# Expert results sent to two rows of each token as slots end, combined by whole-block loads

## The chip, the cores and the metric

The kernel runs on one core of a Trainium2 chip. The metric is device time in microseconds, the median of several executions. One execution was also profiled; its trace gives every instruction's start, length and wait. PE is the matrix engine (PEld its weight loads), DVE the vector engine, ACT the scalar engine, POOL GpSimd and SP the engine that here only issues DMAs.

## The reference, cut to what matters

`x` is 2 x 4096 tokens of 256 floats. An attention-like layer (projections, a decaying running sum, a gate) is added to `x` and normalised; then each token goes through two of eight experts:

```python
x = _layernorm(x + _L0_attn_ref(x, ...))
# _L0_ffn_ref, on the flattened tokens:
logits = x_flat @ gate_W                       # 8 experts
gates = jax.nn.softmax(logits, axis=-1)
tk_g, tk_i = jax.lax.top_k(gates, TOP_K)       # the two best
tk_g = tk_g / (jnp.sum(tk_g, axis=-1, keepdims=True) + 1e-08)
cw = jnp.sum(jax.nn.one_hot(tk_i, E, dtype=x.dtype) * tk_g[..., None], axis=1)
out = x_flat
for e in range(E):
    h = jax.nn.relu(x_flat @ W1[e] + b1[e])    # 256 -> 512
    out = out + cw[:, e:e + 1] * (h @ W2[e] + b2[e])
x = _layernorm(x + out)                        # out begins with x_flat: x counts twice
```

## The kernel before, in words

Tokens are worked in 16 blocks of 512 (`NB`; a block is 4 parts of 128 tokens, `NT`). `attention(i)` (L291) is a generator that does one block in steps; the main loop at the end of the program interleaves the steps of three neighbouring blocks and puts expert work between them (`fill`). PE, DVE, ACT and SP run exactly in the order in which the Python program emits (`IN_ORDER`); POOL's order is made by the scheduler, but each POOL instruction, too, waits for those ahead of it.

A block's first layer ends in `rr` (L358 to L378): attention output plus input, normalised to `x1`, which ACT's queue also stores in HBM as `x1_dram[i]` (L377). A normalisation takes its power -0.5 on POOL (`rstd_of`, L233 to L239, the power is L238): DVE prepares the variance (L237), POOL raises it, DVE and ACT go on. There are 32 such powers in the attention part (`rstd_y`, `rstd_a`) and 16 at the end (`rstd_f`).

The routing part finds each token's two experts (`largest`, L411), counts tokens by expert (L451), and computes for each token and choice a row number in `xs`, a buffer in HBM where each expert has a region of its own. Eight indirect DMAs on POOL (L470) send the block's x1 rows there, one per part and choice, 128 rows of 1 KB each.

The blocks form two groups, 13 and 3 (`GROUPS`). As soon as regions fill, `plan_slots` (L496) plans "slots": 256 consecutive rows of one expert, and once a group is complete, 21 "rest" slots of 128 rows, some of them padding. Group 0 has 45 full slots and 21 rest slots, group 1 has 5 and 21. A slot goes through:

- `load_slot` (L559 on): SP loads the rows (`xg`, L571) and the expert's first weights (`w`, 512 KB, L578), up to three slots ahead;
- `slot_columns`: PE transposes the rows (L590), DVE copies them (`xgT`, L591), ACT copies the expert's second weights from the resident `kept` (L596);
- `slot_first` (L608, ReLU on ACT at L615) and `slot_second` (L629, bias added by DVE at L633 into `ysl`, two buffers);
- `store_slot` (L638): SP stores `ysl` into `ys`, at the same rows as in `xs`.

`half()` does half of this for one slot; `store_slot` comes one half after the slot's result.

When all slots of a group have been stored, its blocks are combined. `gather` (L644 on) loads a part's two expert rows per token by two indirect DMAs on POOL (L654) with the row numbers kept from the routing, and, at a block's first part, SP loads x1 (`sum`, L650). `AHEAD = 3` parts are gathered before one is weighed. `weigh` (DVE) adds both rows times their weights (L669, two instructions) and takes statistics (L675, L676). Then `scale_of` (power on POOL) and `end`: DVE `less` (L687), four ACT instructions (L689), and a store of the block (L693). `some_combining(n)` does n such steps; `half()` sets n in proportion to what is left, so that group 0's combination is spread over group 1's slots. After the last slot only combination is left.

At the start POOL zero-fills padding areas: 14 DMAs of 128 rows (L205) and, when a group is complete, 8 more each after the regions' ends. `lam_sb` holds the decay spread over 512 columns for the running sum (L302), made by two copies (L761).

Of the kernel before, what the change touches and what calls it, by code (L numbers as in the profile page):

```python
# [15 lines left out]
P = 128  # L16
# [4 lines left out]
AHEAD = 3  # L21
# [10 lines left out]
def kernel(  # L32
# [22 lines left out]

    nc = tc.nc
# [18 lines left out]
    KEPT = NF * D + D + NF  # L75
# [5 lines left out]
    lam_sb = const.tile([P, NC, TB], FP, tag="lam", name="lam_sb")  # L81
# [43 lines left out]
    kept = const.tile([P, E, KEPT], FP, tag="kept", name="kept")  # L125

# [29 lines left out]
    m_rows = const.tile([1, MAXS, E], FP, tag="m_rows", name="m_rows")  # L156
    nc.vector.tensor_scalar_mul(m_rows, m_tab, float(SL))

    zeros = const.tile([P, D], FP, tag="zeros", name="zeros")
    nc.gpsimd.memset(zeros, 0.0)  # L160

    class Group:


        def __init__(self, k, n_blocks):
# [7 lines left out]
            self.xs = dram.tile([rows, D], FP, tag=f"xs_{k}", name=f"xs_{k}")  # L173
            self.ys = dram.tile([rows, D], FP, tag=f"ys_{k}", name=f"ys_{k}")
# [10 lines left out]
            self.dumps = const.tile([1, MAXS, E], FP, tag=f"dumps_{k}", name=f"dumps_{k}")  # L185
            nc.vector.tensor_scalar(
                self.dumps, m_tab, float(E - 1 - self.rest), 0.0, ALU.add, ALU.max
# [6 lines left out]
                self.off, m_tab, float(P), self.dumps, ALU.mult, ALU.subtract  # L194
# [9 lines left out]
        def put_zeros(self, row):  # L204
            self.put(nc.gpsimd.dma_start(  # L205
                out=self.xs[ds(row, P), :], in_=zeros
            ))
# [7 lines left out]
        def store(self, dma):  # L215
            key = f"ys_{self.k}"

            tc.declare_no_dep(
                dma.ins, group=key, keep=self.stored[-1:], reason="rows of their own"
            )  # L220
            tc.add_to_no_dep_group(key, dma.ins)
            self.stored.append(dma.ins)

    groups = [Group(k, n) for k, n in enumerate(GROUPS)]
    for m in range(E - 1):
        for gr in groups:
            gr.put_zeros(gr.dump + m * P)
# [45 lines left out]
    def project(w, xT, o, name):  # L273
# [13 lines left out]
        dram.tile([P, NT, D], FP, tag=f"x1_{i}", name=f"x1d_{i}") for i in range(NB)  # L287
# [3 lines left out]
    def attention(i):  # L291
# [7 lines left out]
        for o in range(NC):  # L299
# [4 lines left out]
                lam_sb[:, o, :],  # L304
# [53 lines left out]
        rr = work.tile([P, NT, D], FP, tag="x1", name=f"x1_{i}", bufs=3)  # L358
        for t2 in range(NT // 2):
            o_ps = ps_a.tile([P, 2, D], FP, tag="pa", name=f"ao_{i}_{t2}")  # L360
            for u in range(2):
# [6 lines left out]
                rr[:, 2 * t2 : 2 * t2 + 2, :], o_ps, x_t[:, 2 * t2 : 2 * t2 + 2, :], ALU.add  # L368
# [3 lines left out]
        mv = row_stats(lambda t: rr[:, t, :], f"a{i}")  # L372
        r = rstd_of(mv[:, :, 1:2], f"a{i}")
        yield
        normalise(x1, lambda t: rr[:, t, :], mv, r, f"a{i}")
# [35 lines left out]
        def largest(src, name, hot):  # L411
# [9 lines left out]
            return top  # L421

        hot = small.tile([P, 2, NT, E], FP, tag="hot", name=f"hot_{i}")
        top1 = largest(g, "1", hot[:, 0])
# [3 lines left out]
        top2 = largest(rest, "2", hot[:, 1])  # L428
# [50 lines left out]
    def schedule(gr, j):  # L479
# [3 lines left out]
        if j == gr.n_blocks - 1:  # L483

            ends = small.tile([1, E], I32, tag="s_ends", name=f"ends_{gr.k}")
            nc.vector.tensor_copy(ends, gr.base[:1, :])
            for e in range(E):
                gr.put_zeros(
                    nc.values_load(
                        ends[:, e : e + 1], engines=[ENG.Pool],  # L490
                        min_val=e * gr.cap, max_val=(e + 1) * gr.cap - P,
                    )
                )
            plan_slots(gr, f"{gr.k}_rest", gr.rest, True)

    def plan_slots(gr, name, n, rest):  # L496
# [52 lines left out]
        if rest:  # L549
            nc.vector.tensor_tensor(plan[:, 0, :n, :], at, gr.dumps[:, :n, 0:1], ALU.add)  # L550
        else:
            nc.vector.tensor_copy(plan[:, 0, :n, :], at)
# [7 lines left out]
    def load_slot(s):  # L560
# [8 lines left out]
        xg = slot.tile([P, SL // P, D], FP, tag="xg", name=f"xg_{name}", bufs=3)  # L569
# [13 lines left out]
    def slot_columns(s):  # L583
# [7 lines left out]
        nc.vector.tensor_copy(xgT, pt)  # L591
        e = nc.values_load(
# [4 lines left out]
        return gr, name, size, row, xgT, w1_t, wb[:, 0, :]  # L597

    def slot_first(s):
        gr, name, size, row, xgT, w1_t, wb = s  # L600
        b1_t = wb[:, NF * D + D :]
# [16 lines left out]
        return gr, name, size, row, hT, wb  # L618

    def slot_second(s):  # L620
        gr, name, size, row, hT, wb = s
# [12 lines left out]
        return gr, size, row, y  # L634

    def store_slot(s):
        gr, size, row, y = s
        gr.store(nc.sync.dma_start(  # L638
            out=gr.ys[ds(row, size), :].rearrange("(p t) d -> p t d", p=P), in_=y
        ))  # L640
        left[gr.k] -= size // P
        if left[gr.k] == 0:
            to_gather.extend((i, t) for i in place if place[i][0] is gr for t in range(NT))

    def gather(i, t):

        gr, _ = place[i]
        if t == 0:
            sums[i] = work.tile([P, NT, D], FP, tag="sum", name=f"sum_{i}", bufs=3)
            nc.sync.dma_start(out=sums[i], in_=x1_dram[i])  # L650
        both = []
        for k in range(2):
            yk = work.tile([P, D], FP, tag=f"y{k}", name=f"y{k}_{i}_{t}", bufs=AHEAD + 2)
            dma = nc.gpsimd.indirect_dma_start(  # L654
                out=yk.bitcast(I32),
                out_offset=None,
                in_=gr.ys.bitcast(I32),
                in_offset=bass.IndirectOffsetOnAxis(ap=poss[i][:, k, t, :], axis=0),
            )
            for ins in gr.stored:  # L660
                tc.add_manual_dep(dma.ins, ins.name, SYNC, reason="rows stored before")
            both.append(yk)
        return i, t, both

    def weigh(i, t, both):
# [183 lines left out]
```

## Time and profile before

| what | value |
|---|---|
| median of 3 executions | 1097.53 us (1095.64 to 1101.23) |
| the profiled execution's own time | 1091.48 us |
| its span, first to last instruction | 1089.5 us |
| PE busy | 899.7 us, 83% |
| DVE busy | 548.4 us, 50% |
| ACT busy | 386.1 us, 35% |
| POOL busy | 318.5 us, 29% |
| moved by DMA | 163.79 MB, 150 GB/s over the span |
| L470, indirect DMA out of x1 | 128 times, 972 ns each on POOL |
| L654, indirect DMA into y | 128 times, 981 ns each on POOL |
| L669, weighing, DVE | 128 times, 481 ns each |
| L238, power, POOL | about 1.0 us each |
| L633, `ysl`, DVE | 686 ns for a full slot |

"Busy" is the time in which the engine worked; for POOL's indirect DMAs it is the time to issue them, not that of the transfer. A row of the groups by line gives line, engine, operation, output and inputs, count, then busy time and mean duration, then the engine's idle time before and what ended it. In the timeline a line gives start, length, engine, line, operation and, in brackets, idle time before it and what ended that.

### The profile page before, as it was taken

The page shows a single profiled execution, that of the slowest core. Times are in us where ns is not written, and L with a number is a line of the kernel's source. Part 1 is how long each engine was busy: PE and PEld are TensorE (multiplying, and loading weights), DVE is VectorE, ACT ScalarE, POOL GpSimd, SP SyncE. Part 2 cuts the span into 40 slices and gives each one's busy share as a digit, 9 for nine tenths or more (in the row PEclk, how much of TensorE's full clock was granted, in tenths as well). Part 3 has the DMA queues.
Part 4 walks back from the last instruction along what each step waited for, and adds up shares of the span by engine and source line. Part 5 has one row for each costly group of instructions (what it writes and reads, how often), then busy time and mean ns, then how long its engine had stood idle before and what let it go on. Part 6 is the DMA issues. An engine that isn't in the chain of part 4 may idle for free. (4 is left out here: it accounts for less than half of the span.)

```text
span 1089.5 us, 14838 instructions
## 1 busy us (share of the span) xinstructions
PE 899.7 (83%) x4366; PEld 713.7 (66%) x4366; DVE 548.4 (50%) x1841; ACT 386.1 (35%) x733; POOL 318.5 (29%) x346
## 2 busy tenths in 40 slices
PE   4988586899899999999999999999898965776710
PEld 2555354778677777778786868688797854666610
DVE  2675544356455554555455455534334245665544
ACT  1221212323333334343333323334454423554412
POOL 3112321302030303030211203130304367676454
PEclk9998796999999999999999999999899988888965
DMA  5611214232333424242434342443647857988653
GB/s 192 205 54 44 88 60 143 99 124 88 133 119 126 151 101 161 94 151 88 146 102 131 112 131 97 164 155 128 193 155 226 269 182 246 281 296 267 229 175 110
DMA packets 95041, 163.79 MB, mean 150 GB/s; under 512 B 12081, under 2 KB 45361, under 8 KB 94961
## 3 DMA queue, kind: packets, MB, share of 16 engines
q1 hardware_dynamic: 68800, 107.52, 30.6%
q0 software_dynamic: 13728, 37.50, 10.4%
q10 hardware_dynamic: 12432, 17.84, 4.5%
q8 instruction: 34, 0.56, 0.2%
q14 instruction: 47, 0.38, 0.1%
HBM read 106.72 MB, written 56.10 MB: 149 GB/s over the span
## 5 line engine op out<-in xcount | busy, mean ns | idle before, releaser
L629 PE MATMUL po<-wb,hT 128*128 128x256 f32 x800 | 190.3, 393 | 8.1 <-issue 6.2
L608 PE MATMUL ph<-xgT,w 128*128 128x256 f32 x800 | 185.8, 386 | 10.4 <-DVE xgT L591 10.4
L608 PEld LDWEIGHTS ph<-xgT,w 128*128 128x128 f32 x800 | 154.1, 194 | 36.9 <-DVE xgT L591 11.2
L629 PEld LDWEIGHTS po<-wb,hT 128*128 128x128 f32 x800 | 153.6, 197 | 29.7 <-issue 7.1
L470 POOL DMA_INDIRECT xs<-x,pos x128 | 124.4, 972 | 142.8 <-DVE rows L512 102.1
L615 ACT ACTIVATE hT<-ph,wb 128x256 f32<-128x256 f32 x200 | 83.9, 471 | 211.3 <-PE ph L608 149.8
L654 POOL DMA_INDIRECT y<-ys,pos x128 | 125.5, 981 | 81.3 <-issue 29.9
L238 POOL TENSOR_TENSOR rstd_a<-rstd_a,half_neg 128x4 f32<-128x4 f32 x16 | 16.1, 1007 | 429.5 <-DVE rstd_a L237 429.5
L629 PE MATMUL po_rest<-wb_rest,hT_rest 128*128 128x256 f32 x336 | 89.6, 415 | 18.0 <-DVE rstd_f L237 12.8
L608 PE MATMUL ph_rest<-xgT_rest,w_rest 128*128 128x128 f32 x672 | 89.3, 290 | 18.2 <-DVE xgT_rest L591 12.4
L591 DVE COPY xgT<-xt 128x512 f32<-128x512 f32 x50 | 34.5, 691 | 137.1 <-PE xt L590 110.1
L608 PEld LDWEIGHTS ph_rest<-xgT_rest,w_rest 128*128 128x128 f32 x672 | 86.9, 204 | 24.1 <-DVE xgT_rest L591 14.2
L615 ACT ACTIVATE hT_rest<-ph_rest,wb_rest 128x128 f32<-128x128 f32 x168 | 48.1, 369 | 116.3 <-PE ph_rest L608 45.8
L629 PEld LDWEIGHTS po_rest<-wb_rest,hT_rest 128*128 128x128 f32 x336 | 67.0, 210 | 29.1 <-issue 16.3
L633 DVE TENSOR_TENSOR ysl<-po,wb 128x512 f32<-128x512 f32 x50 | 34.3, 686 | 85.9 <-PE po L629 33.5
L276 PE MATMUL g<-xT,wg_sb 128*128 128x512 f32 x128 | 61.4, 621 | 8.4 <-DVE state L302 5.0
L596 ACT COPY wb<-kept 128x1284 f32 x50 | 63.1, 1262 | 3.8 <-DVE ysl L633 0.9
L669 DVE SCALAR_TENSOR_TENSOR sum<-y,wt,sum 128x256 f32<-128x256 f32 x128 | 61.5, 481 | 5.5 <-DMA y<-ys,pos 3.3
L276 PE MATMUL q<-xT,wq_sb 128*128 128x512 f32 x128 | 59.7, 610 | 0.4 <-ACT yg L351 0.4
L276 PE MATMUL v<-xT,wv_sb 128*128 128x512 f32 x128 | 59.5, 609 | 0.3 <-issue 0.3
L363 PE MATMUL ao<-wo_sb,yg 128*128 128x256 f32 x256 | 58.2, 380 | 0.9 <-DVE y L326 0.9
L596 ACT COPY wb_rest<-kept 128x1284 f32 x42 | 53.5, 1275 | 5.0 <-DVE ysl_rest L633 3.6
(143 smaller groups left out, 1097.9 us busy)
## 6 DMA issues: line engine op xcount, KB each, us to landing
w<-in_w_dram SPq DMA_DIRECT2D x50, 512.0 KB
w_rest<-in_w_dram SPq DMA_DIRECT2D x42, 512.0 KB
xg<-xs SPq DMA_DIRECT2D x50, 256.0 KB
ys<-ysl SPq DMA_DIRECT2D x50, 256.0 KB
x<-in_x_dram SPq DMA_DIRECT2D x16, 512.0 KB
x1d<-x ACTq DMA_DIRECT2D x16, 512.0 KB
sum<-x1d SPq DMA_DIRECT2D x16, 512.0 KB
out_dram<-sum ACTq DMA_DIRECT2D x16, 512.0 KB
```

The source lines that it names most:

```text
L238: nc.gpsimd.tensor_tensor(r, r, half_neg[:, :n, :], ALU.pow)
L276: last = nc.tensor.matmul(ps, w[:, c, ts(o, P)], xT[:, c, :], start=(c == 0), stop=(c == NC - 1))
L363: nc.tensor.matmul(o_ps[:, u, :], yg[:, c, ts(2 * t2 + u, P)], wo_sb[:, c, :], start=(c == 0), stop=(c == NC - 1),)
L470: gr.put(nc.gpsimd.indirect_dma_start(out=gr.xs, out_offset=bass.IndirectOffsetOnAxis(ap=pos[:, k, t, :], axis=0), in_=x1s[i][:, t, :], in ...
L591: nc.vector.tensor_copy(xgT, pt)
L596: nc.scalar.copy(wb, kept[:, ds(e, 1), :])
L608: nc.tensor.matmul(ph[:, u, :], w1_t[:, c, ts(f0 + u, P)], xgT[:, c, :], start=(c == 0), stop=(c == NC - 1),)
L615: nc.scalar.activation(hT[:, f, :], ph[:, u, :], AF.Relu, bias=b1_t[:, f : f + 1])
L629: nc.tensor.matmul(po[:, t, :], hT[:, f, ts(t, P)], w2_t[:, f, :], start=(f == 0), stop=(f == NF - 1),)
L633: nc.vector.tensor_tensor(y, po, b2_t.broadcast_to([P, n_t, D]), ALU.add)
L654: dma = nc.gpsimd.indirect_dma_start(out=yk.bitcast(I32), out_offset=None, in_=gr.ys.bitcast(I32), in_offset=bass.IndirectOffsetOnAxis(ap= ...
L669: nc.vector.scalar_tensor_tensor(x1[:, t, :], yk, wt[:, k, t, :], x1[:, t, :], ALU.mult, ALU.add)
```

## The change

Each row in `xs` now carries eight more floats (`ROW = D + 8`, 1056 bytes). Float 0 of them is twice the token's number in its group, float 1 tells the token's first expert as `E - e`. The first is written by DVE for each block (from a table made once by POOL), the second is a copy in the routing part. `x1_dram` has the wide rows too. `xs`, its padding included, holds valid numbers everywhere: padding rows carry numbers of spare rows behind the tokens' own. The spare rows are made once in HBM (`no_rows`) and copied from there; filling at the start takes six larger POOL DMAs in place of 14.

`ys` has two rows for each token, first and second choice reversed (`1 - k` at weighing). A slot copies the two floats out of `xg` (`whose`, DVE), and after its result computes the target row (`to`, DVE): twice the token's number, plus one if the slot's expert is the token's first. `kept` has one more float per expert for that comparison. `store_slot` sends the result by indirect DMAs on POOL, one per 128 rows, and no longer through SP.

`gather` is gone. `load_sum` loads, for a whole block, x1 and both rows of each token by two plain DMAs on SP, the second of 1 MB after all stores of the group. It does so while at most one block is waiting to be weighed, with two buffers for the rows. The pace is computed with a load as one step.

`lam_sb` is gone; the running sum reads one column repeated. Tables of the planner are smaller.

```diff
+    ROW = D + 8
-    KEPT = NF * D + D + NF
+    KEPT = NF * D + D + NF + 1
...
+    for e in range(E):
+        nc.vector.memset(kept[:, e, KEPT - 1 :], float(E - e))
...
+    def put_none(rows, k, n):
+        rows = rows.rearrange("(n p) d -> p n d", p=P)
+        return (
+            nc.gpsimd.dma_start(out=rows[:, :, :D], in_=zeros.broadcast_to([P, n, D])),
+            nc.gpsimd.dma_start(out=rows[:, :, D:], in_=none[:, k : k + n, :]),
+        )
+    no_rows = dram.tile([E * P, ROW], FP, tag="no_rows", name="no_rows")
+    put_none(no_rows, 0, E)
...
-        def put_zeros(self, row):
-            self.put(nc.gpsimd.dma_start(
-                out=self.xs[ds(row, P), :], in_=zeros
-            ))
+        def put_none(self, row, e):
+            self.put(nc.gpsimd.dma_start(out=self.xs[ds(row, P), :], in_=no_rows[ts(e, P), :]))
...
-            tc.declare_no_dep(
-                dma.ins, group=key, keep=self.stored[-1:], reason="rows of their own"
-            )
+            tc.declare_no_dep(dma.ins, group=key, reason="rows of their own")
...
-                lam_sb[:, o, :],
+                lam_col[:, o : o + 1].broadcast_to([P, TB]),
...
+        rr = work.tile([P, NT, ROW], FP, tag="x1", name=f"x1_{i}", bufs=3)
+        nc.vector.tensor_scalar_add(rr[:, :, D:], number, float(2 * TB * place[i][1]))
...
+        top1, first = largest(g, "1", hot[:, 0])
+        nc.vector.tensor_copy(x1[:, :, D + 1 : D + 2], first)
...
         nc.vector.tensor_copy(xgT, pt)
+        whose = slot.tile([P, SL // P, 2], FP, tag="whose", name=f"whose_{name}", bufs=4)
+        whose = whose[:, : size // P, :]
+        nc.vector.tensor_copy(whose, xg[:, : size // P, D : D + 2])
...
         nc.vector.tensor_tensor(y, po, b2_t.broadcast_to([P, n_t, D]), ALU.add)
-        return gr, size, row, y
+        to = slot.tile([P, SL // P, 1], I32, tag="to", name=f"to_{name}")[:, :n_t, :]
+        nc.vector.scalar_tensor_tensor(
+            to, whose[:, :, 1:2], wb[:, KEPT - 1 :], whose[:, :, 0:1], ALU.is_equal, ALU.add
+        )
+        return gr, size, to, y
...
-        gr.store(nc.sync.dma_start(
-            out=gr.ys[ds(row, size), :].rearrange("(p t) d -> p t d", p=P), in_=y
-        ))
+        for t in range(size // P):
+            gr.store(nc.gpsimd.indirect_dma_start(
+                out=gr.ys,
+                out_offset=bass.IndirectOffsetOnAxis(ap=to[:, t, :], axis=0),
+                in_=y[:, t, :],
+                in_offset=None,
+            ))
...
-    def gather(i, t):
...
+    def load_sum(i):
+        gr, j = place[i]
+        x1 = work.tile([P, NT, ROW], FP, tag="sum", name=f"sum_{i}", bufs=3)
+        nc.sync.dma_start(out=x1, in_=x1_dram[i])
+        y2 = work.tile([P, NT, 2, D], FP, tag="y2", name=f"y2_{i}")
+        dma = nc.sync.dma_start(
+            out=y2,
+            in_=gr.ys[ts(j, 2 * TB), :].rearrange("(t p k) d -> p t k d", t=NT, p=P),
+        )
+        for name in gr.stored:
+            tc.add_manual_dep(dma.ins, name, SYNC, reason="rows stored before")
+        sums[i] = x1
+        to_weigh.extend((i, t, y2) for t in range(NT))
...
-            if to_gather:
-                gathered.append(gather(*to_gather.pop(0)))
-            if len(gathered) > AHEAD or (gathered and not to_gather):
-                weigh(*gathered.pop(0))
+            if to_load and len(to_weigh) <= NT:
+                load_sum(to_load.pop(0))
+            elif to_weigh:
+                weigh(*to_weigh.pop(0))
...
-        debt[0] += len(to_gather) * size / (P * max(1, 2 * sum(left.values()) - 8))
+        todo = 5 * len(to_load) + len(to_weigh)
+        debt[0] += todo * size / (P * max(1, 2 * sum(left.values()) - 8))
```

## The prediction, made before the changed kernel ran

> **What bounds the kernel now.** I read the stretches first, since the program has stages with different limits (columns: the stretch and its length, busy us and instruction count of PE, PE's weight loads, DVE, ACT and POOL, then granted clock, DMA share, GB/s).
>
> ```profile
> 300.00:600.00 300.00, 288.92 (x1386) 228.40 (x1385) 157.67 (x549) 108.02 (x193) 58.87 (x60) 1.00 0.37 124
> 600.00:830.00 230.00, 214.85 (x1167) 182.75 (x1166) 109.51 (x409) 92.70 (x180) 50.98 (x56) 0.97 0.44 145
> 860.00:890.00 30.00, 20.97 (x88) 17.52 (x87) 11.75 (x31) 7.15 (x14) 19.98 (x21) 0.83 0.64 212
> 920.00:950.00 30.00, 18.46 (x104) 15.68 (x102) 14.79 (x42) 13.21 (x28) 21.06 (x21) 0.86 0.87 283
> 950.00:980.00 30.00, 22.17 (x117) 19.25 (x118) 19.39 (x56) 17.48 (x37) 20.87 (x21) 0.80 0.86 281
> 1010.00:1040.00 30.00, 23.38 (x140) 20.46 (x138) 14.86 (x42) 13.78 (x30) 12.02 (x12) 0.94 0.57 189
> 1040.00:1089.50 49.50, 0.00 (x0) 0.00 (x0) 23.94 (x70) 10.37 (x20) 27.64 (x28) 0.54 0.48 151
> ```
>
> Three stages. Up to about 857 us ("front") PE is 93 to 96% busy and nothing near the change can give more than a few per cent. From 857 to 1040 ("window") group 0's blocks are combined beside group 1's slots: PE works only 126.6 of 180 us (the six 30-us stretches summed) and DMA is the fullest resource, 0.84 to 0.87 in the middle. From 1040 ("tail") PE has ended; 49.5 us go to group 1's combination.
>
> The groups by line, then the tail's timeline, tell what the tail waits for:
>
> ```profile
> L470 POOL DMA_INDIRECT xs<-x,pos x128 | 124.4, 972 | 142.8 <-DVE rows L512 102.1
> L654 POOL DMA_INDIRECT y<-ys,pos x128 | 125.5, 981 | 81.3 <-issue 29.9
> L669 DVE SCALAR_TENSOR_TENSOR sum<-y,wt,sum 128x256 f32<-128x256 f32 x128 | 61.5, 481 | 5.5 <-DMA y<-ys,pos 3.3
> ```
> ```profile
> 1042.79 1.01 POOL L654 DMA_INDIRECT y<-ys,pos  x1 [12.96 <-DMA ys<-ysl_rest]
> 1044.10 0.97 POOL L654 DMA_INDIRECT y<-ys,pos  x1 [0.30 <-issue]
> ...
> 1046.40 0.48 DVE L669 SCALAR_TENSOR_TENSOR sum<-y,wt,sum 128x256 f32<-128x256 f32 x1 [1.35 <-DMA y<-ys,pos]
> ...
> 1082.79 2.07 ACT L689 ACTIVATE sum<-sum,less,rstd_f 128x256 f32<-128x256 f32 x4 [4.23 <-DVE less L687]
> ```
>
> A gather occupies POOL 0.96 us and the next follows 0.30 us later, 1.26 us each. 24 of them are 30 us of the tail, and DVE follows at their pace. In the window 104 gathers are 131 us of POOL, while SP's own waits name the store:
>
> ```profile
> SPq L638 <- DVE ysl_rest L633: 14.3, 8, 2.8
> SPq L638 <- DMA ys<-ysl_rest: 7.8, 7, 2.3
> ```
>
> All waits of L638 there sum to 35.8 us (14.3, 7.8, 6.2, 3.0, 1.9, 1.7, 0.9), with later weight and row loads queued behind it on SP. The window also opens with a hole: PE's transpose at 879.62 waited 7.14 us for rows whose load SP issued at 857.81, while 14 gathers were issued.
>
> **What the Trainium skill says.** "DMA: Bandwidth & Descriptors", section "Issuing engines are not separate DMA queues": transfers of SP, ACT and POOL run on the same 16 engines and interleave. The trace agrees: in 860 to 1040 the three queues take 41.6, 25.1 and 9.1% of them, so a gather replaced by a plain load of the same bytes frees POOL, not DMA. Same page, "Anatomy of one DMA — SWDGE (gpsimd) path": a small DMA's time is mostly its receipt. Here a gather's rows are used 2.2 to 2.6 us after its issue ended (1045.07 to 1047.26 and 1043.80 to 1046.40). Same page, "Measured (HBM→SBUF, 128 partitions, SWDGE, issued from GpSimd)": 1 MB from HBM takes 6.15 us; no 1 MB load is in this trace, whose best short stretches move 340 to 350 GB/s. Same page, "How a descriptor splits into AXI transactions": an unaligned start costs extra beats, up to 7 on the 33 of a 1056-byte row; no such row is in the trace of before.
>
> **The change part by part.** Account: span 1089.5 us, execution 1091.5 us, 6 us under the median of 1097.5; I carry differences over to the median.
>
> *Tail, removed and added.* Removed are 24 gathers. Added: the last scatter and three block loads. The last slot's result is ready at 1040.0. The row number on DVE (like L687, 0.17 us), a scatter on POOL (0.96, the row of L470), landing 2.4 us (middle of the gathers'), SP's issue 0.4: the first block's rows start at 1044.0. Block load 6 us (the page's price; 4.5 to 8, from 350 GB/s plus landing, up to sharing with the x1 load): 1050.0. One part of a block on DVE takes 1.57 us in the tail (two of L669, statistics 0.43 and 0.18, gaps), a block 6.3: block 13 ends at 1056.3. Block 14 was loaded behind it: ends 1062.6. Block 15 reuses block 13's buffer (two are kept), so its load starts at 1056.4 and lands at 1062.7: ends 1069.0. Variance, power, `less` 1.5; then ACT and the last store as now (1082.79 to 1089.5, 6.7): 1077.2. Gain 12 us, 8 to 16 with the load's bounds.
>
> *Window.* Bytes stay: 104 gathers of 128 KB become 13 block loads of 1 MB; the stores become scatters of equal size; x1 and xs rows grow by 3%. One block's share is about 1.05 (y) + 0.54 (x1) + 0.52 (out) + 2.1 slots of 0.79 MB = 3.8 MB, at 283 GB/s 13.3 us; it now takes 180/13 = 13.8. DVE's part per block is 6.3 + 2.6 (slots) + waiting for the power; about 12 us, so DMA stays the bound. What can improve is filling: SP no longer waits in L638, its loads come earlier, and slot results leave through POOL's queue instead of standing behind weight loads. I take 300 GB/s (the 283 measured, times 0.92 over 0.87): 12.7 us a block, some 8 us over the saturated 126 us (886 to 1012). The opening hole becomes another: the first block load waits for the last scatter's landing, and behind it on SP stand the next slots' loads; DVE's first weighing waits for it, and behind that stand xgT copies that PE needs. I price it at 5 us against 7. Gain 10 us; at best 25 (hole gone, DMA at the 318 GB/s of its best 4 us), at worst 13 lost (14.8 us a block: a whole block must land before its first row is weighed, where a gather pair was enough).
>
> *Front.* Added are scatters for 45 full slots and 21 halves: 111 x 1.26 = 140 us on POOL, which is busy 159 of 770 us. POOL works in order; the 32 powers (L238) stand behind them, DVE waits for a power, PE for DVE. In the block at 476 us the result is ready at 477.07 and the power at 479.4; by the built order the four scatters of two slots stand ahead, ending at 480.0: 0.5 us late. At 458 the order leaves the power unhindered. So about 0.25 us per power on DVE, 8 us over 32, of which PE's buffers hide more than half: 3 us; nothing at best, 40 if each power is late by a whole scatter. The scatters hold no semaphore long: each waits for the landing of the POOL DMA eight before it. DVE gets 92 copies of the row's tail and 92 row numbers, with 32 small ones 216 x 0.17 = 36 us, beside PE: DVE is 53% busy, and PE waited for it only some 16 us of 300 to 850; 0 to 6, taken within the 3. The xs scatters (37 to 44% DMA share) hide wider rows. SP's loads wait for the tail copy too; that follows the xgT copy directly, 0.
>
> *Start.* 14 zero-fills become six larger POOL DMAs of 22 x 128 rows of 1 KB and as many of 32 bytes. Their issue is not shown: 0.54 us each if flat (3 us), 0.54 per 128 rows if not (24 us), starting at 3. POOL then idles until the first power at 32.68, so both ends are covered; extra traffic beside the first weights 0 to 3 us; I take 0. The two `lam_sb` copies lie before a 3.09-us wait for PE: 0. Padding rows now copied within HBM: eight small issues as before, 0.
>
> Sum: -12 - 10 + 3 = -19 us: span 1070, median 1079.
>
> **The rivals.** (A) As worked: 1079. (B) Better filling: the window gives 25 and the tail 15 with the front at 3: -37, 1061. For it speaks SP's 35.8 us of waiting; against it that PE is not held by SP alone. (C) DMA stays as it fills now: window 0, tail 10, front 4: 1091. For it speaks that bytes do not fall; against it the 0.64 and 0.57 stretches. (D) Slower: scatters ahead of the powers on POOL. Place: 60 to 850 us; price 1.26 us per scatter ahead; if every power is one scatter late and PE feels it, 32 x 1.26 = 40 us less 22: 1116. It decides from (22 + 5.5)/32 = 0.86 us of mean lateness felt by PE. For it speaks that the front has PE at 96%, so losses are not absorbed; against it the order at 458 and 476 us.
>
> **How the numbers follow.** About 0.5% (5.5 us) is what a measurement can tell from no change. A 0.45, B 0.17, C 0.18, D 0.20. Faster by over 0.5%: A, B and a part of C, 0.66; same 0.13; slower 0.21. Range 1061 to 1106: B's centre to a D with 0.95 us of lateness, which also takes in the window's loss of 13 with a front of 10 or so.
>
> **What would show it.** In the after profile: tail from PE's end near 37 us with no gathers; window shorter by about 10 us with DMA near 0.9; PE in 300 to 600 still about 289 us; `less_y` and `yn` waiting for POOL hardly more. PE's share in the front falling below 93%, with DVE waiting for L238's power, would be D. A DVE wait for y at each block's first weighing with window unchanged would be C.

## The result and the profile after

The changed kernel takes 1125.57 us (median of 4, 1124.49 to 1127.53), the kernel before beside it 1096.59 us (4 runs, 1093.73 to 1101.23): a ratio of 1.0262, 95% interval 1.0223 to 1.0302. It is slower by 29 us; 1079 us, a gain of 18, was forecast. Later runs fell on other chips of the same kind, and there the ratio was another one; the experiments come to that. The profiled execution took 1124.49 us, its span is 1122.9 us, 33.4 more than before.

The stretches first, of the changed kernel (columns as in the prediction: busy us and count of PE, weight loads, DVE, ACT, POOL, then granted clock, DMA share, GB/s):

```profile
300.00:600.00 300.00, 275.00 (x1240) 216.00 (x1240) 146.69 (x539) 96.26 (x172) 89.92 (x92) 0.95 0.34 110
985.00:1015.00 30.00, 20.64 (x128) 17.79 (x127) 20.09 (x65) 16.90 (x37) 7.62 (x8) 0.94 0.92 303
1045.00:1075.00 30.00, 24.30 (x155) 21.77 (x154) 23.58 (x76) 18.08 (x40) 8.07 (x8) 0.94 0.98 329
1081.50:1122.90 41.40, 0.02 (x1) 0.00 (x0) 19.56 (x58) 8.30 (x16) 5.37 (x6) 0.56 0.48 159
```

The two stages that the change is about did get better: the window is 20 us shorter, with a DMA share of 0.82 to 0.98 in the 30-us stretches from 925 to 1075 (two are shown; before it was 0.84 to 0.87 in the middle), and the tail after PE's end is 41.4 us instead of 50.0. The front got worse: in 300 to 600 PE is 275 of 300 us busy instead of 289, at a clock of 0.95 instead of 1.00. I put the two spans side by side at four marks of the traces: the first v matmul, the end of the last block's counting matmul (`n`), PE's end, the span's end.

| stage | before | after | difference |
|---|---|---|---|
| start, to the first v matmul | 16.4 | 20.6 | +4.2 |
| front, to the last `n` | 802.2 | 860.2 | +58.0 |
| window, to PE's end | 221.0 | 200.7 | -20.3 |
| tail | 50.0 | 41.4 | -8.6 |

The start and the front lose 62 us and the other two give 29 back. From one v matmul to that of the next block the front takes 57.3 to 57.9 us in most blocks, where it took 51.2.

The groups by line of the changed kernel:

```profile
L670 POOL DMA_INDIRECT ys<-ysl,to x100 | 98.3, 983 | 322.3 <-DVE to L662 243.4
L292 PE MATMUL pt_x<-ident,x 128*128 128x128 f32 x256 | 39.7, 291 | 39.6 <-DVE state L324 31.1
```

A scatter (L670) costs POOL what was assumed. The new item is in the second line: PE stands 31.1 us idle ahead of transposes of the next blocks, waiting for the running sum. The waits of PE in 300 to 700, before and then after (us in total, number of waits, longest):

```profile
PE pt_x L270 <- DVE state L302: 10.3, 8, 1.4
```
```profile
PE pt_x L292 <- DVE state L324: 31.1, 7, 4.6
```

Once per block, 4.6 us at the longest instead of 1.4. Why the sum is late shows in one block's timeline (start, length, engine, line, operation; in brackets the idle time ahead and what ended it). Before:

```profile
470.48 0.60 PE L590 MATMUL xt<-ident,xg 128*128 128x128 f32 x4
471.11 0.69 DVE L591 COPY xgT<-xt 128x512 f32<-128x512 f32 x1 [2.88 <-PE ph L608]
470.91 3.62 PE L629 MATMUL po<-wb,hT 128*128 128x256 f32 x16
476.38 0.69 DVE L633 TENSOR_TENSOR ysl<-po,wb 128x512 f32<-128x512 f32 x1 [4.58 <-PE yt L336]
473.81 0.96 POOL L470 DMA_INDIRECT xs<-x,pos  x1 [0.31 <-issue]
479.34 2.44 DVE L302 TENSOR_TENSOR_SCAN state<-lam_sb,state,v 128x512 f32<-128x512 f32 x2
```

and after:

```profile
499.23 0.60 PE L613 MATMUL xt<-ident,xg 128*128 128x128 f32 x4
504.50 0.69 DVE L614 COPY xgT<-xt 128x512 f32<-128x512 f32 x1 [7.28 <-PE yt L358]
499.67 3.62 PE L655 MATMUL po<-wb,hT 128*128 128x256 f32 x16
508.28 0.69 DVE L659 TENSOR_TENSOR ysl<-po,wb 128x512 f32<-128x512 f32 x1 [3.01 <-issue]
502.55 0.96 POOL L494 DMA_INDIRECT xs<-x,pos  x1 [0.30 <-issue]
503.81 0.96 POOL L670 DMA_INDIRECT ys<-ysl,to  x1 [0.31 <-issue]
505.07 0.96 POOL L670 DMA_INDIRECT ys<-ysl,to  x1 [0.30 <-issue]
511.37 2.44 DVE L324 TENSOR_TENSOR_SCAN state<-lam_col,state,v 128x512 f32<-128x512 f32 x2
512.70 0.80 PE L292 MATMUL pt_x<-ident,x 128*128 128x128 f32 x4 [4.25 <-DVE state L324]
```

Read DVE against PE. `xgT` needs only the `xt` transposes, whose end is at 499.83; it starts at 504.50. `ysl` needs `po`, ended at 503.29; it starts at 508.28, 5 us late, and the block's statistics and the scan stand behind it on DVE. Before, `xgT` was on time and `ysl` 1.8 us late (`po` ended at 474.53). DVE has nothing else to do in these gaps: the signal that PE is done comes late. The trace's own records of PE's signals say the same: those of matmuls that ended at 503.29 to 508.45 come in one bunch, 0.06 us apart, from 508.20 to 508.50, while PE itself worked on. In both kernels that happens behind the row of eight scatters of a block's rows (L470, L494). Before, the signals are through 1.5 us after the row's last scatter, in block after block; after the change two scatters of a slot follow without a pause, and the signals are through about 2.2 us after the last of ten. ACT is held as well: `hT` needs a matmul that ended at 499.40 and starts at 500.90. I call this the hold.

One thing more follows the stall. Stretches of the changed kernel:

```profile
508.10:512.70 4.60, 0.35 (x2) 0.13 (x2) 4.25 (x13) 0.58 (x1) 2.89 (x3) 1.00 0.81 210
513.10:516.50 3.40, 3.40 (x11) 2.74 (x10) 1.67 (x4) 1.51 (x3) 0.00 (x0) 0.50 0.59 223
526.70:530.10 3.40, 3.40 (x10) 2.66 (x9) 2.92 (x18) 0.00 (x0) 0.00 (x0) 0.50 0.00 0
```

PE's clock is halved twice for 3.4 us, each worth 1.7 us: right behind the stall, and again right behind `lg`, 16 narrow matmuls of the routing. So it goes in most blocks; in the kernel before it is 1.00 throughout 300 to 700. The stall's growth (4.25 - 1.39 = 2.9) and two halvings (3.4) make 6.3 of the 6.6 us by which this period is longer (57.87 against 51.23).

The tail, answering to the gathers shown before:

```profile
1082.38 0.96 POOL L670 DMA_INDIRECT ys<-ysl_rest,to_rest  x1 [0.71 <-DVE rstd_f L259]
1085.03 0.37 SPq L686 DMA_DIRECT2D y<-ys  x1
1090.78 1.00 DVE L699 SCALAR_TENSOR_TENSOR sum<-y,wt,sum 128x256 f32<-128x256 f32 x2 [6.17 <-DMA y<-ys]
1113.37 2.07 ACT L720 ACTIVATE sum<-sum,less,rstd_f 128x256 f32<-128x256 f32 x4 [4.24 <-DVE less L718]
```

It runs as foreseen: last scatter, one load of 1 MB (5.4 us from the end of its issue to its use), three blocks at DVE's pace.

### The profile page after: what moved, and what is told of

It reads as the page before. It is cut to its first block, busy times and chain, and to the rows that moved or that the text cites. A ratio compares the mean times of both kernels' runs of the same rounds, so it can differ in the third digit from the quotient of the medians.

```text
span 1122.9 us, 14659 instructions
## 1 busy us (share of the span) xinstructions
PE 919.1 (82%) x4366; PEld 724.9 (65%) x4366; DVE 568.5 (51%) x2063; ACT 385.5 (34%) x733; POOL 329.1 (29%) x355
## 4 chain that ended last, share of the span: by engine, by line
PE 61%; DVE 13%; issue 8%; DMA 8%; POOL 4%; ACT 3%; SPq 1%; another core or an unknown queue 0%; ACTq 0%; POOLq 0%; DVEq 0%
PE po L655 15%; PE ph L634 14%; PE ao L386 5%; PE q L298 5%; PE po_rest L655 4%; PE g L298 4%; PE ph_rest L634 4%; DMA xg_rest<-xs 3%; PE lg L410 3%; DVE sum L699 3%; POOL xs L494 2%; PE pt_x L292 2%; PE xt L613 2%; PE v L298 2%; DVE bnst_f L706 1%
## 5 line engine op out<-in xcount | busy, mean ns | idle before, releaser
L655 PE MATMUL po<-wb,hT 128*128 128x256 f32 x800 | 202.9, 412 | 12.1 <-ACT hT L641 4.8
L634 PE MATMUL ph<-xgT,w 128*128 128x256 f32 x800 | 196.3, 402 | 12.1 <-DVE xgT L614 10.5
L670 POOL DMA_INDIRECT ys<-ysl,to x100 | 98.3, 983 | 322.3 <-DVE to L662 243.4
L634 PEld LDWEIGHTS ph<-xgT,w 128*128 128x128 f32 x800 | 162.2, 205 | 41.8 <-DVE xgT L614 11.3
L655 PEld LDWEIGHTS po<-wb,hT 128*128 128x128 f32 x800 | 162.4, 208 | 37.4 <-ACT hT L641 5.1
L494 POOL DMA_INDIRECT xs<-x,pos x128 | 123.2, 963 | 62.4 <-issue 26.8
L634 PEld LDWEIGHTS ph_rest<-xgT_rest,w_rest 128*128 128x128 f32 x672 | 81.7, 194 | 16.7 <-DVE xgT_rest L614 8.9
L670 POOL DMA_INDIRECT ys<-ysl_rest,to_rest x42 | 41.1, 979 | 136.0 <-DVE to_rest L662 91.2
L292 PE MATMUL pt_x<-ident,x 128*128 128x128 f32 x256 | 39.7, 291 | 39.6 <-DVE state L324 31.1
L292 PEld LDWEIGHTS pt_x<-ident,x 128*128 128x128 f32 x256 | 31.7, 149 | 52.4 <-DVE state L324 33.4
L622 ACT COPY wb<-kept 128x1285 f32 x50 | 63.3, 1265 | 4.7 <-issue 3.1
```

The lines of the kernel that those rows point to most:

```text
L292: nc.tensor.transpose(pt[:, ts(t, P)], src[:, t, ts(c, P)], ident)
L494: gr.put(nc.gpsimd.indirect_dma_start(out=gr.xs, out_offset=bass.IndirectOffsetOnAxis(ap=pos[:, k, t, :], axis=0), in_=x1s[i][:, t, :], in ...
L622: nc.scalar.copy(wb, kept[:, ds(e, 1), :])
L634: nc.tensor.matmul(ph[:, u, :], w1_t[:, c, ts(f0 + u, P)], xgT[:, c, :], start=(c == 0), stop=(c == NC - 1),)
L655: nc.tensor.matmul(po[:, t, :], hT[:, f, ts(t, P)], w2_t[:, f, :], start=(f == 0), stop=(f == NF - 1),)
L670: gr.store(nc.gpsimd.indirect_dma_start(out=gr.ys, out_offset=bass.IndirectOffsetOnAxis(ap=to[:, t, :], axis=0), in_=y[:, t, :], in_offset ...
```

## The experiments

Three theories for the front. HOLD: as just said; the length of an unbroken row of scatters on POOL decides. BUFFER: `ysl` has two buffers and waits for the scatters of the slot two before. POWERS: the prediction's rival D, powers standing behind scatters on POOL. The first four experiments ran on a chip that behaved as in the two profiles (the kernel before: 1096.04 us, 7 runs).

### Three buffers

```diff
...
-        y = slot.tile([P, SL // P, D], FP, tag="ysl", name=f"ysl_{name}")
+        y = slot.tile([P, SL // P, D], FP, tag="ysl", name=f"ysl_{name}", bufs=3)
```

> The changed kernel with three buffers of the slot's output tile ysl (and of its row numbers) in place of two; room for it is made by one buffer in place of two for two tables of the plan that only VectorE uses. Theory BUFFER (the front is slower because ysl waits until the scatters of the slot two before have landed, and the y statistics and the scan queue behind it on VectorE): the wait goes, the front's period falls from 57.9 us to 51 to 53 us, the median to 1045 to 1070 us. Theory HOLD (while POOL issues scatters back to back, PE's completions reach VectorE and ScalarE late, until about 2 us after the last scatter of the row; the change makes the row ten or twelve scatters long instead of eight): no buffer is in it, period 57 to 58.5 us, median 1120 to 1130 us. Theory POWERS (the powers on POOL come late behind scatters): unchanged too, 1120 to 1130 us.

1123.37 us, ratio 1.0257 (1.0216 to 1.0299): nothing changed, BUFFER falls for the front's period. PE's wait in 300 to 700 is that of the changed kernel:

```profile
PE pt_x L292 <- DVE state L324: 31.4, 7, 4.6
```

### The scatters apart

```diff
...
         next(older, None)
+        hold[0] = i < NB          # slots that end here are kept back ...
         fill(10)
...
         next(old, None)
+        hold[0] = False
+        put_back()                # ... and scattered behind the power emitted last
         fill(1 if i > FEW else 0)
```

> As the run with three ysl buffers, and the two scatters of the slot that ends just before the eight scatters of a block's rows are held back: they are issued behind the power of the y statistics, so that the row on POOL is eight long again and its followers come apart from it. The number of scatters is the same. Theory HOLD: xgT and ysl start on time or within 1.5 us as in the kernel before, period 51.5 to 53.5 us, median 1055 to 1080 us. Theory BUFFER: the same as with three buffers alone, whatever that gives. Theory POWERS: the power stands behind two scatters in place of four, so at most half of the front's loss goes: 1095 to 1115 us.

1077.78 us (4 runs), ratio 0.9835 (0.9801 to 0.9868): 46 us less than with three buffers alone, and faster than the kernel before, with just as many scatters. The front's period is 51.5 or 51.6 us in all but one of the steady blocks. PE's wait is nearly the old one:

```profile
PE pt_x L294 <- DVE state L326: 12.3, 7, 1.8
```

On POOL the row is eight long again. The next scatter, that of a slot which ends later, comes 3 us behind it; the two scatters that were kept back follow the power:

```profile
478.88 0.96 POOL L496 DMA_INDIRECT xs<-x,pos  x1 [0.30 <-issue]
482.85 0.96 POOL L683 DMA_INDIRECT ys<-ysl,to  x1 [3.01 <-DVE to L664]
484.11 0.96 POOL L683 DMA_INDIRECT ys<-ysl,to  x1 [0.30 <-issue]
485.13 1.04 POOL L262 TENSOR_TENSOR rstd_y<-rstd_y,half_neg 128x4 f32<-128x4 f32 x1
486.45 1.03 POOL L683 DMA_INDIRECT ys<-ysl,to  x1 [0.28 <-POOL rstd_y L262]
```

The power still stands behind two scatters here, so POWERS, which allowed for half of the loss at most (1095 us or more), does not explain the 46 us.

### The kernel before with two more scatters

```diff
...
+        for t in range(2):
+            dma = nc.gpsimd.indirect_dma_start(
+                out=junk[gr.k],
+                out_offset=bass.IndirectOffsetOnAxis(ap=pos[:, 0, t, :], axis=0),
+                in_=zeros, in_offset=None,
+            )
...
         schedule(gr, j)
```

> The kernel before with two more scatters per block on POOL right behind the eight of the block's rows: a constant tile of zeros to rows of a tensor that nobody reads. No ysl, no VectorE operation, no wide row, no store is changed; the output is complete. Theory HOLD: the row is ten long, xgT and ysl on VectorE start 2 to 5 us later, PE waits for the scan at pt_x for some 4 us per block, the period rises from 51.2 to 54 to 58 us, the median to 1135 to 1180 us. Theories BUFFER and POWERS: nothing waits for these scatters, and the next power on POOL comes 6 us after the row of eight, which leaves room for 2.5 us: 1095 to 1101 us.

1154.44 us, ratio 1.0534 (1.0492 to 1.0577): two scatters per block that nobody waits for, on an engine that then idles 5 us, cost 58 us in all, and the period is 55.8 to 57.6 us. The same picture as in the changed kernel, without its buffers, its DVE work or its wide rows:

```profile
500.76 0.96 POOL L481 DMA_INDIRECT junk<-zeros,pos  x1 [0.30 <-issue]
503.80 0.69 DVE L645 TENSOR_TENSOR ysl<-po,wb 128x512 f32<-128x512 f32 x1 [7.58 <-PE pt_x L274]
507.00 1.04 POOL L242 TENSOR_TENSOR rstd_y<-rstd_y,half_neg 128x4 f32<-128x4 f32 x1 [5.29 <-DVE rstd_y L241]
508.09 0.97 PE L274 MATMUL pt_x<-ident,x 128*128 128x128 f32 x4 [4.39 <-DVE state L306]
```

`ysl` starts 2.1 us after the end of the last scatter (2.2 in the changed kernel); the power waits for DVE and not the other way round. This is the run that shows added scatters alone to make such a loss; together with the scatters kept apart it shows the hold to be the main cause.

### Plain stores in the changed kernel

```diff
-        for t in range(size // P):
-            gr.store(nc.gpsimd.indirect_dma_start(out=gr.ys, ...))
+        at = next_row[gr.k]
+        next_row[gr.k] += size
+        gr.store(nc.sync.dma_start(
+            out=gr.ys[at : at + size, :].rearrange("(p t) d -> p t d", p=P), in_=y
+        ))
```

> The changed kernel with its slots stored by plain DMAs on SP in the order in which they end, as in the kernel before, no scatters of outputs; wide rows, the extra VectorE operations, the larger start fills and the whole block loads stay. It leaves out that an output row gets to its token, so the sums take other rows of the same size and number. HOLD, BUFFER and POWERS alike: the front has its old period, 51.2 to 52.2 us, and the total is that of before less the gain of window and tail (some 23 and 9 us) plus 4 us of the start: 1065 to 1078 us. A theory that the other parts of the change slow the front: period over 55 us, 1105 to 1125 us.

1065.75 us, ratio 0.9708 (0.9671 to 0.9746), period mostly 51.5 us: the wide rows, the extra DVE operations and the block loads cost the front little, 6.6 us (808.8 against 802.2). With the scatters apart the front takes 816.2 us, and that run is 12 us longer than this one. So the 58 us of the front are some 7 of these other parts, some 7 of the scatters even when they stand apart, and 44 of their standing right behind the eight, by these single profiles.

### Late fills, a pause, four more

These four ran on another chip (the kernel before: 1090.88 us, 15 runs). The fills moved to later blocks, on top of the scatters apart:

> As the run with the scatters kept apart, and the three pairs of fills on POOL at the start (the rows for no token, and the dummy rows behind xs of both groups) are issued in the blocks 4 to 6 instead of ahead of the first block. Theory: at the start they stand before the small loads of ln_g and ln_b on the DMA engines, for which VectorE waits in order, so the first v matmul came 4.3 us later; expected: it comes at 16 to 17 us again, as in the kernel before, and the median falls by 3 to 5 us against the run kept apart (1077.8): 1072 to 1076 us. Rival: something else in the start (the longer list of constants on POOL and VectorE) holds it: no change, 1076 to 1080 us.

1076.95 us, ratio 0.9858 (0.9814 to 0.9903). This edit did not do what it says: nothing tied the fills to a later step, and the scheduler left them at 3.26 to 9.27 us on POOL, the first v matmul at 20.4. It is a repeat of the scatters apart, and agrees with it.

The row of eight cut in two, in the kernel before:

```diff
...
+                if (t, k) == (1, 1):
+                    fourth = dma.ins.name
+                if t >= 2:
+                    tc.add_manual_dep(dma.ins, rest_op, SYNC, reason="a pause")
+            if t == 1:
+                idle = stat("idle")
+                for _ in range(1):
+                    op = nc.gpsimd.tensor_tensor(idle, wt[:, 0], half_neg, ALU.pow)
+                    tc.add_manual_dep(op.ins, fourth, SYNC, reason="a pause")
+                    rest_op = op.ins.name
```

> The kernel before, with its row of eight scatters per block cut in two rows of four: the fifth waits for one power on POOL (1.04 us) that waits until the fourth has landed. Theory HOLD with a row's length as the cause: neither row reaches the point at which PE's completions get late (about 6 us into a row), ysl after the row starts on time instead of 1.8 us late, PE does not wait at pt_x, its clock is not cut: the period falls from 51.2 to 47.5 to 50 us, the median to 1055 to 1085 us. If the time since the first scatter or the number of scatters counts, and not the row without a pause: the hold ends some 3.5 us later than before, the period rises to 53 to 57 us and the median to 1115 to 1165 us.

1092.20 us (12 runs), ratio 1.0012 (1.0002 to 1.0022). Neither expectation. The hold is gone: up to 785 us no signal of PE comes late, `ysl` starts 0.1 us after `po`, PE never waits for the scan. So it is not the number of scatters in a block that counts, but a row of them without a break. (The break lets the earlier ones land; whether the row on POOL or the number of transfers under way is what counts was not told apart.) But the period stays 51.3 us. The stretch tells where the gain went:

```profile
300.00:600.00 300.00, 297.11 (x1394) 236.04 (x1393) 156.47 (x530) 110.02 (x198) 65.49 (x66) 0.97 0.37 126
```

PE is busy for 297 of 300 us instead of 289, but at 0.97 of its clock: one halving of 3.4 us per block, always right behind `lg`, has taken the place of the 1.4 us stall, so that taking it out gained nothing here.

The same pause in the run with late fills:

> The run with late fills, and the row of eight cut in two rows of four by the same pause. Theory HOLD with a row's length as the cause: xgT and ysl start on time, the front loses 1 to 3 us per block against the run with late fills, median 1035 to 1068 us. If the number of scatters counts, or if the pause pushes the next scatters and the power behind them: 1075 to 1110 us.

1078.38 us, ratio 0.9872 (0.9837 to 0.9907). The time lies in the range of the other expectation, 1075 to 1110, but the trace does not show its reasons: rows of four, five and six scatters, and up to 750 us only four late signals, by 0.1 to 1.0 us. HOLD's gain fails as before: the period is 51.3 us at a clock of 0.98.

Four more scatters in place of two in the kernel before:

> The kernel before with four more scatters per block of a constant tile right behind the eight, to rows that nobody reads (the run with two more had a period of 57.4 us and 1154 us). Theory HOLD: the row is twelve long and ends 2.5 us later than with ten; each microsecond past the point where PE needs the scan costs one and some loss of clock: period 59 to 62 us, 1180 to 1220 us. If the row of ten was a single threshold: 57 to 58 us, 1150 to 1160 us.

1189.09 us (one run), periods of 58.4 to 60.3 us: as HOLD says, the row of twelve costs more than that of ten. In all the traces with the hold the first late signal between 180 and 750 us comes 5.7 us or more after a row began.

### Chips without the hold

The later runs fell on three further chips. On all three the kernel before took 1050 to 1064 us (medians 1058.91, 1059.61 and 1059.48, 23 runs each), not 1091 to 1097. What their profiles show of the hold: none. I counted the signals of PE in each trace that come over 0.05 us after the end of any matmul that gives one: 81 of 669 in the kernel before and 72 of 645 in the changed one as first profiled, none of 712 and none of 688 here (the two at a program's end left out). In each of the two first traces 41 of PE's signals have no record at all; here none is missing. Whether the recording of a trace has a part in the hold no run tells. Each chip was used at one time only, those with the hold first: that the chip makes the difference, and not something else that changed between these times, is likely but not shown.

> The changed kernel unchanged, beside the kernel before on the same chip. On a chip with the hold (the kernel before at 1088 to 1101 us and its ysl behind a row of eight 1.8 us late): 1120 to 1130 us, a ratio of 1.022 to 1.030. On a chip without it (the kernel before at 1052 to 1063 us): the scatters of a row cost nothing in the front, which then has a period of 51.3 us; the window's gain is gone too, because the kernel before has no hold by its gathers there; the start costs 4 us and the tail gives 8: 1050 to 1062 us, a ratio of 0.99 to 1.003. If the front's loss were of another kind than the hold (buffers, powers, VectorE's queue), it would be there on every chip: a ratio of 1.02 to 1.03 again.

1065.97 us (20 runs) beside 1059.61 (23): ratio 1.0070 (1.0049 to 1.0091), above the expected 0.99 to 1.003. A block of the changed kernel there:

```profile
478.75 3.62 PE L655 MATMUL po<-wb,hT 128*128 128x256 f32 x16
482.46 0.69 DVE L659 TENSOR_TENSOR ysl<-po,wb 128x512 f32<-128x512 f32 x1 [2.74 <-issue]
482.88 0.96 POOL L670 DMA_INDIRECT ys<-ysl,to  x1 [0.31 <-issue]
486.68 0.96 POOL L670 DMA_INDIRECT ys<-ysl,to  x1 [0.30 <-issue]
486.52 1.04 PE L292 MATMUL pt_x<-ident,x 128*128 128x128 f32 x8
```

Here both slots' scatters follow the eight without a pause, a row of twelve from 472.78 to 487.64; `ysl` starts 0.1 us after `po` in the middle of it, and PE waits for nothing. The period is 51.3 us. In these blocks twelve scatters cost nothing where there is no hold.

> The kernel before unchanged, for its profile on this chip. With the hold: ysl behind the row of eight 1.8 us late, 1088 to 1101 us. Without it: ysl on time, PE does not wait at pt_x, one cut of the clock of 3.4 us per block instead, the window some 25 us shorter, 1052 to 1063 us.

1053.26 us (one run), span 1051.7. Its window, from the last `n` to PE's end, is 195.1 us; in the kernel before as first profiled it is 221.0. The changed kernel has 198.2 here and 200.7 there. So the 20 us that the change gained in the window are, by these single profiles, what the hold took from the kernel before, whose gathers are rows on POOL too: 44 of its 81 late signals come after the last `n`, 2 of 72 in the changed kernel. Where there is no hold, nothing is gained. The tail gives 8.7 us here (50.0 to 41.4), the start costs 4.1.

The front is not free here either: 790.0 us before, 805.7 after. This run of the kernel before is a short one, 6 us under its median, and three of its blocks take 49.6 us without stall or halved clock; by the medians some 8 us remain (an estimate: 6.4 in all, less 4.1 and 3.1, plus 8.7). Of the 15.7 us, 8.8 come after the last v matmul (130.2 against 139.0). In the changed kernel two lines stand there that tell why in part:

```profile
797.19 0.42 DVE L659 TENSOR_TENSOR ysl_rest<-po_rest,wb_rest 128x256 f32<-128x256 f32 x1 [5.69 <-DMA ys<-ysl_rest,to_rest]
797.67 2.58 PE L655 MATMUL po_rest<-wb_rest,hT_rest 128*128 128x256 f32 x7 [2.98 <-DVE ysl_rest L659]
```

Scatters of rest slots stand on POOL behind a block's eight, and `ysl_rest`, with the two buffers of `ysl`, waits for their landing (once more in the window, for 7.0 us). That is BUFFER, in a place where the periods do not show it. How the rest of the front's loss comes about was not found.

The fills tied to powers of the blocks 4 to 6, on the scatters apart:

```diff
...
+        for dma in both:
+            tc.add_manual_dep(dma.ins, after, SYNC, reason="not at the start")
```

> As the run with late fills, whose six fills still stood at the start on POOL because nothing tied them to a later step; here each waits for a power of the blocks 4 to 6. If the fills delay the small loads of ln_g and ln_b at the start: the first v matmul at 16 to 17 us instead of 20.4, median 1071 to 1075 us (run kept apart: 1077.8, run with late fills: 1077.0). If the start is late for another reason: 1076 to 1079 us.

1055.18 us (20 runs), ratio 0.9962 (0.9943 to 0.9980), on a chip without the hold; the first v matmul at 13.2 us, earlier than in the kernel before. The same kernel once more, on another chip:

> The version with the scatters apart and the fills moved to the blocks 4 to 6. On a chip with the hold: the scatters apart gave 1077.8 us there with the first v matmul at 20.1 us; with it at 13.2 us, as measured on the chip without the hold, 1068 to 1074 us, a ratio of 0.974 to 0.982. On a chip without the hold: a ratio of 0.994 to 0.998 again.

1056.24 us (20 runs), ratio 0.9981 (0.9959 to 1.0003), without the hold again. Scatters apart and fills later is thus the best complete version I have, though the second interval just takes in no change: on chips with the hold its form with early fills is at 0.984 and 0.986 of before, on those without it this one is at 0.996 and 0.998. With late fills it was not measured on a chip with the hold.

Two kernels were to tell number from bytes, and scatters from a busy POOL: two more scatters of narrow rows (`zeros[:, :32]`), and two powers in their place.

> The kernel before with two more scatters per block of rows of 128 bytes instead of 1024, behind the eight. POOL is as long about each (some 0.96 us), the bytes are an eighth. If the number of scatters (or of rows) in a row makes the hold: the same as with the two wide ones, period 57 us, 1145 to 1160 us. If the bytes that the scatters write make it: period 51 to 53 us, 1095 to 1115 us.

> The kernel before with two powers of 128x4 (1.04 us each) on POOL behind the eight scatters of each block, whose result nobody reads: POOL is busy as long as with two more scatters, without a DMA. If a busy POOL late in the block were the cause (the power of the y statistics behind it): period 57 us, 1145 to 1160 us. If it is the scatters: as before, 51.2 us and 1088 to 1098 us.

1072.15 and 1068.05 us on a chip without the hold, period 51.3 us in both. They can't tell what they were made for. Both kernels were measured twice more:

> The kernel before with two more scatters per block of rows of 128 bytes, once more. On a chip with the hold: 57 us period and 1145 to 1160 us if the number of scatters counts, 51 to 53 us and 1090 to 1115 us if the bytes count. On a chip without it: a period of 51.3 us and 1055 to 1075 us, which tells nothing of it.

> The kernel before with two powers on POOL behind the eight scatters, once more. On a chip with the hold: 57 us period if a busy POOL makes the loss, 51.2 us and 1088 to 1100 us if the scatters make it. On a chip without it: 51.3 us and 1055 to 1070 us.

> The kernel before with two more scatters per block of rows of 128 bytes. On a chip with the hold (the kernel before at 1088 to 1101 us): 57 us period and 1145 to 1160 us if the number of scatters counts, 51 to 53 us and 1090 to 1115 us if the bytes count. On a chip without it (the kernel before at 1052 to 1063 us): about 1070 us, as twice before.

> The kernel before with two powers on POOL behind the eight scatters. On a chip with the hold: 57 us period if a busy POOL makes the loss, 51.2 us and 1088 to 1101 us if the scatters make it. On a chip without it: about 1067 us, as twice before.

1069.66, 1067.30, 1069.16 and 1064.13 us, one run each, without the hold both times. Beside the medians of the kernel before on these chips (1058.91 to 1059.61), the scatters cost 10 to 13 us and the powers 5 to 9: something is lost to a busier POOL here too, outside of the steady blocks. Open stays whether the number of scatters, their bytes or a POOL that is merely busy make the hold, and whether PE's results come late or only the news of them.

## Why the prediction was wrong

The forecast's step that failed is **the front**, priced at 3 us (40 at worst); it cost 58 in the profile after. That step asked only what stands behind a scatter on POOL, found the powers, and saw that they would be 0 to 0.5 us late. That much was right: in 300 to 700 DVE's waits for a power of the y statistics stay below 1 us in all, before and after. The cost came by a way that the step left out, and so put at nothing: what a longer row of scatters does to others' signals, 44 of the 58 us by the runs above. The profile of before showed it, in a wait that I passed over:

```profile
DVE ysl L633 <- PE yt L336: 31.8, 7, 4.6
```

`ysl` waits for `po`; here it is released by a signal of `yt`, a later matmul, in seven blocks. A releaser that comes after the one needed says that the needed signal was late. Read with the row of scatters next to it, that was the warning.

**Rival D** had the direction, the place and nearly the size (1116 us, with 0.20), and the wrong mechanism: its sign in the profile was to be PE's share below 93% with DVE waiting for powers; the share fell to 92%, the waits for powers did not come. The scatters kept apart and the two idle scatters separate the two.

**The start**, put at 0, cost 4.2 us. POOL's time for the six fills was nearer its lower end, some 1.0 us each. The traffic, taken as 0 of 0 to 3 us, was the term that was too small: the loads of `ln_g` and `ln_b`, for which DVE waits in order ahead of the decay, landed at 16.4 and 18.1 us instead of both by 13.4. Tying the fills to later blocks brought the first v matmul to 13.2.

**The window**, put at -10, gave 20.3, near its good end of 25, but not by what I named: SP's waiting for stores was to be the cause, and on a chip without the hold the window gives nothing (195.1 to 198.2). That it fell within its range was luck.

**The tail**, put at -12 (8 to 16), gave 8.6. The first block's rows, the 1 MB load (6 us taken, after the price in the Trainium skill, "DMA: Bandwidth & Descriptors", section "Measured (HBM→SBUF, 128 partitions, SWDGE, issued from GpSimd)"; 5.4 measured on SP's queue) and 6.4 us per block on DVE were as worked out. Missing were `less` of a block waiting 1.2 us for its power ahead of the next block's weighing, and the last store: 7.5 us from ACT's end to the span's end instead of 4.7. Its source now has gaps between rows; whether that is why was not tried.

**Without the hold** the forecast fails too: 6.4 us were lost and not 18 gained. There the window's step is the one that is furthest off (3.1 us lost, 10 forecast as gained), then the front with some 8 for 3, and the start.

Two readings of the profile before were off, too. PE is 93 to 96% busy from 300 to 830 us, not from the start: in 60 to 300 it is 197.09 of 240 us, 82%. And 318 and 350 GB/s are not the best rates on record there: 331 stand for 898 to 902 us, and 410 for 10 to 12 us. Neither is the step that failed.

## What to carry to other kernels

Price a DMA issued by an engine not only by who is queued behind it there, but by the length of the unbroken row that it joins: in some runs here a row of ten scatters kept other engines from hearing of PE for 5 us, and a pause of 3 us took most of that cost away. When a wait is ended by something later than what it needs, ask what was held up. And before a stall is taken out, see whether the clock takes it back; before a result is believed, see it on a second chip.

## What the runs showed of the hardware

- Rows of eight to twelve indirect DMAs on POOL, 1.26 us apart, delayed PE's signals to DVE and ACT until 1.5 to 2.0 us (row of eight) or 2.0 to 2.4 us (row of ten) after the last one, in the first two profiles and on the first two chips of the experiments; on the three others rows of eight, ten and twelve delayed none. A row of four, ended by its landing and one power, delayed none up to 785 us even where the hold is.
- PE's clock was halved for 3.4 us at a time. In ten traces every halving between 300 and 700 us came right behind 3.4 us in which PE had mostly stood still (busy for 0 to 1.1 us) or behind the 16 narrow matmuls of `lg` (3.4 us with PE busy for 2.9 to 3.0). The second kind came in most blocks where PE had no stall (297 of 300 us busy, period 51.3 us, on chips with and without the hold; three blocks of one profile went without, at 49.6 us each) and where the stall was 4.3 us. With a stall of 1.4 us per block neither kind came. What rule stands behind that the runs do not tell.
